# A q store in one transfer, and the sums moved to the middle of a unit

## The chip, the cores and the metric

The kernel runs on one core of a Trainium2 chip. The metric is the device time of one execution in microseconds. Three runs of the kernel before gave 3701.26, 3701.26 and 3703.98, a median of 3701.26.

## What is computed

Eight images of 256 channels and 64x64 pixels go through two layers, all in float32. The first is an attention block whose keys and values come from a 4x4 strided convolution. The second is a linear attention, and only it is touched here (cut to what matters):

```
qkv = einsum('oc,bchw->bohw', w_qkv, x)
dw  = conv5x5_depthwise(qkv, w_dw)
agg = einsum('goi,bgihw->bgohw', w_pw, dw.reshape(B, G, 8, H, W)).reshape(B, G * 8, H, W)
ms  = concatenate([qkv, agg], axis=1)
q, k, v = relu(ms's first 8 of 24), relu(next 8), last 8 with a 1 appended
kv  = einsum('bhnd,bhne->bhde', k, v)
out = einsum('bhnd,bhde->bhne', q, kv); out = out[..., :-1] / (out[..., -1:] + 1e-15)
return x + batchnorm(einsum('oc,bchw->bohw', w_proj, out))
```

So half of the heads ("raw") take q, k and v from qkv itself, and the other half ("agg") from its depthwise 5x5 convolution mixed 8x8 per group.

## The kernel before

Three passes follow each other. **The first pass** computes the attention block and qkv, image by image, and writes qkv to scratch in DRAM: q and k as planes of cells by phase (`planes`), k and v again with tokens on partitions (`kd`, `vd`). Beside that, `conv_weights` (L674) multiplies the convolution's taps by the mixing weights and stores them as matrices (`wtd`), so that the convolution is a matrix product later. For q (j = 0, 1, nine matrices per group) the columns of such a matrix are ordered with the phase f (16 of them) outside and the channel o (8) inside. `wb` is the product (L690) and L698 and L700 store it.

**The second pass** (L1140) goes over 64 units: two halves t, four blocks k of 32 channels, and eight images b, the image innermost. A unit makes

- the raw sums (`summed_raw`, L1361): k times v on TensorE, 32 products of 32 columns, 128x32 (L1367), which read the keys `kq` after their relu and the tokens `vq`;
- the k convolution in three products, `convolve(u, 2)`, `(u, 0)` and `(u, 1)` (L1290, matmuls at L1298), whose results leave PSUM through ScalarE (`both`, L1307), the vector engine (`s`, L1314) and a relu into `r` (L1315);
- the sums of convolved k with v, for the unit before (`summed`, L1377): 32 products of 288 columns (L1384), which read that `r` and the same `vq`, followed by a reduction on GpSimd (`reduced`, L1276, tile `red_agg`) and small work on the vector engine (L1394 to L1401);
- a column of counts for each (`ended_raw`, L1404, and `ended`, L1418), one small product each.

Two units make one convolution of q, for two images at once: nine products (`product`, L1318, matmuls at L1329) are spread over the even and the odd unit that come two units later, in three parts each (`products`, L1439). They read the cells `d` (L1186), differences of columns (`across`, L1227, vector engine) and of rows (`down`, L1240; vector engine L1248 and GpSimd L1249). `finished` (L1334) writes the relu of the result into `r`, a tile with partitions (f, o), four groups h and two images i. `stored` (L1428) writes it to `qd`, which has channels first and phases second, so that each group h of each image is a transfer of its own: eight of 128 KB for two images.

All transfers are issued on SyncE's queue in order. `load_tokens` (L1194) issues one transfer for `kq` and eight for `vq`; `kq` has two buffers and `vq` three, and the third is freed by `summed`. The framework orders each engine's instructions by the order of the code and by when it thinks that their inputs are there, so the issued order can differ from that of the code; `tc.keep_in_program_order` pins an instruction behind the one traced before it on its engine. The small stores and most q stores on SyncE are pinned in this way. PSUM has five buffers for the convolutions (`cv`) and one each for the raw sums, the sums and the counts.

The loop of a unit, without its loads and stores, is this before the change (p = u-1, q = u-2):

```
summed_raw(u)
across(q // 2, 0); down(q // 2, 1)        # even units
summed(p)
convolve(u, 2); paired(u + 1)
products(u, 0); convolve(u, 0); ended_raw(u)
products(u, 1); convolve(u, 1)
ended(p); products(u, 2); positive(u + 1)
```

**The third pass** loads q back (`agg`, L1564), divides and projects. It reads `qd` in the same layout before and after.

Of the kernel before, what the change touches and what calls it, by code (L numbers as in the profile page):

```python
# [27 lines left out]
F32 = mybir.dt.float32  # L28
AF = mybir.ActivationFunctionType
ALU = mybir.AluOpType  # L30
AX = mybir.AxisListType

P = 128
# [8 lines left out]
D0 = C // HEADS  # L42
D1 = 8
# [531 lines left out]
def first_pass(ctx: ExitStack, tc: tile.TileContext, a, fine, planes, x2d, kd, vd, wtd):  # L575
    nc = tc.nc
# [6 lines left out]
    made = ctx.enter_context(tc.tile_pool(name="made", bufs=1))  # L583
# [23 lines left out]
    consts, x_tiles = {}, {}  # L607
# [66 lines left out]
    def conv_weights():  # L674
        for j, half in ((j, half) for j in (2, 3, 0, 1) for half in range(2)):
            n = 6 if j > 1 else 9
            wd = made.tile([P, 8, n, 16], F32, tag="wd", name=f"wd_{j}_{half}", bufs=1)
            src = a.w_big[:, j, 8 * half : 8 * half + 8]
            nc.sync.dma_start(wd[:, :, :4], src.rearrange("p g (n f) -> p g n f", n=4))
            yield  # L680

            tc.keep_in_program_order(nc.vector.tensor_add(wd[:, :, 4:6], wd[:, :, 0:4:2], wd[:, :, 1:4:2]))
            if n == 9:
                tc.keep_in_program_order(nc.vector.tensor_add(wd[:, :, 6:8], wd[:, :, 0:2], wd[:, :, 2:4]))
                tc.keep_in_program_order(nc.vector.tensor_add(wd[:, :, 8], wd[:, :, 4], wd[:, :, 5]))
            for i in range(8):
                g = 8 * half + i
                w = made.tile([P, n * 16, D1], F32, tag="wb", name=f"wb_{j}_{g}", bufs=1)
                tc.keep_in_program_order(
                    nc.vector.tensor_tensor(  # L690
                        w,
                        wd[:, i].rearrange("p n f -> p (n f)").unsqueeze(2).to_broadcast([P, n * 16, D1]),
                        consts["wsmall"][:, j, g].unsqueeze(1).to_broadcast([P, n * 16, D1]),
                        ALU.mult,
                    )
                )
                if n == 6:
                    nc.sync.dma_start(wtd[j][:, g], w.rearrange("p n o -> p (n o)"))  # L698
                else:
                    nc.sync.dma_start(  # L700
                        wtd[j][:, :, g].rearrange("n p o -> p n o"), w.rearrange("p (n f) o -> p n (f o)", n=n)
                    )
                yield


# [348 lines left out]
    n_all = len(order)  # L1054
    todo = {}
    for n in range(n_all + 6):
        now, was = n < n_all, 0 <= n - 1 < n_all
# [12 lines left out]
        if was:  # L1070
            p = order[n - 1]
# [24 lines left out]
        if was and p[2]:  # L1096
            b, s = p[:2]
# [42 lines left out]
def second_pass(ctx: ExitStack, tc: tile.TileContext, a, planes, kd, vd, wtd, kvd, kvg, qd, ahead):  # L1140
    nc = tc.nc
# [16 lines left out]
    def bank(tag, name, bufs=1, n=512):  # L1158
        return psums[tag].tile([P, n], F32, tag=tag, name=name, bufs=bufs)

    units = [(t, k, b) for t in range(2) for k in range(4) for b in range(B)]
    n_all = len(units)
# [120 lines left out]
    def positive(u):  # L1283
        kq = kqs[u]
        tc.keep_in_program_order(nc.scalar.activation(kq, kq, AF.Relu))
        reduced(u, "raw", (kq[:, 0], kq[:, 1]))
# [74 lines left out]
    def summed_raw(u):  # L1361
        kq, vq = kqs.pop(u), vqs[u]
        ps = bank("raw", f"raw_{u}")
        for i in range(8):
            r, c = i // 4, i % 4
            for f in range(4):
                nc.tensor.matmul(  # L1367
                    ps[f * D0 : (f + 1) * D0, :D0],
                    kq[:, r, c, f * D0 : (f + 1) * D0],
                    vq[:, r + 1, c + 1, f].rearrange("p h e -> p (h e)"),  # L1370
                    start=(i == 0),
                    stop=(i == 7),
                )
        raws[u] = ps


    def summed(u):  # L1377
        kt, vq = kts.pop(u), vqs.pop(u)
        kt = kt.rearrange("p q h (n e) -> p q h n e", n=4)
        ps = bank("sums", f"sums_{u}")  # L1380
        for i in range(8):
            par, r, c = i // 4, i // 2 % 2, i % 2
            for h in range(4):
                nc.tensor.matmul(  # L1384
                    ps[h * D0 : (h + 1) * D0, : 36 * D1].rearrange("p (r n e) -> p r n e", r=3, e=D1),
                    kt[:, par, h, 2 * r + c],
                    vq[:, r : r + 3, 2 * par + c : 2 * par + c + 3, :, h].rearrange("p r c f e -> p r (c f) e"),
                    start=(i == 0),
                    stop=(i == 7),
                )  # L1390
        t, k, b = units[u]
        reduced(u, "agg", (kt[:, 0].rearrange("p h n e -> p n h e"), kt[:, 1].rearrange("p h n e -> p n h e")))
        p = small.tile([P, 36, D1], F32, tag="p", name=f"p_{u}", bufs=1)
        nc.vector.tensor_mul(p, ps[:, : 36 * D1].rearrange("p (n e) -> p n e", e=D1), taps[t][:, k])  # L1394
        s = small.tile([P, D1], F32, tag="kv", name=f"kv_{u}")
        nc.vector.tensor_reduce(s, p.rearrange("p n e -> p e n"), AX.X, ALU.add)

        x = small.tile([P, D1, D1], F32, tag="mixed", name=f"mixed_{u}")
        nc.vector.tensor_mul(x, mix[:, 4 * t + k], s.unsqueeze(1).to_broadcast([P, D1, D1]))
        m = small.tile([P, D1 + 1], F32, tag="m", name=f"m_{u}")  # L1400
        nc.vector.tensor_reduce(m[:, :D1], x, AX.X, ALU.add)  # L1401
        maggs[u] = m

    def ended_raw(u):  # L1404
        t, k, b = units[u]
        ps = raws.pop(u)
        col = ps[:, 64:65]
        nc.tensor.matmul(col, reds.pop((u, "raw")), ones, start=True, stop=True)
        m = small.tile([P, D0 + 1], F32, tag="mraw", name=f"mraw_{u}")
        nc.vector.tensor_copy(m[:, :D0], ps[:, :D0])  # L1410
        nc.vector.tensor_copy(m[:, D0:], col)
        mraws[u] = m

    def stored_raw(u):
        t, k, b = units[u]
        tc.keep_in_program_order(nc.sync.dma_start(kvd[b, t][:, k], mraws.pop(u)))
# [11 lines left out]
    def stored(m):  # L1428
        r = quad.pop(m).r
        for i in range(2):  # L1430
            t, k, b = units[2 * m + i]
            for h in range(4):
                c0 = P * t + D0 * k + D1 * h
                put = nc.sync.dma_start(qd[b][c0 : c0 + D1].rearrange("d f n -> f d n"), r[:, h, i])  # L1434

                if 2 * m + i < n_all - 3:
                    tc.keep_in_program_order(put)

    def products(u, part):  # L1439
        m, odd_one = divmod(u - 2, 2)  # L1440
# [7 lines left out]
    for u in range(n_all + 3):  # L1448
        p, q = u - 1, u - 2
        now, was, conv = u < n_all, 0 <= p < n_all, 0 <= q < n_all  # L1450
        if u == n_all - 5:
            next(ahead)
        if 0 < u < n_all:
            summed_raw(u)
        if 1 < u < n_all - 1:
            load_tokens(u + 1)
        if u % 2 and u < n_all:
            load_cells_q(u // 2)
        if was:
            stored_raw(p)  # L1460
        if conv:
            stored_agg(q)
        if u % 2 == 0 and u > 2:
            stored(u // 2 - 2)
        if u == n_all - 3:
            next(ahead)
        if conv and u % 2 == 0:
            across(q // 2, 0)
            down(q // 2, 1)
        if was:  # L1470
            summed(p)
        if now:
            convolve(u, 2)
        if u + 1 < n_all:
            paired(u + 1)
        if u == n_all - 1:
            next(ahead)
        if u == n_all:
            next(ahead)
        if u == n_all + 1:  # L1480
            ahead.send(lambda name: bank("cv", name, 5))
        if conv and u % 2:
            down(q // 2, 2)
        products(u, 0)
        if now:
            convolve(u, 0)
            if u == 0:
                summed_raw(u)
            ended_raw(u)
        if conv and u % 2 == 0:  # L1490
            down(q // 2, 0)
            across(q // 2, 2)
        products(u, 1)
        if now:
            convolve(u, 1)
        if u + 2 < n_all:
            load_cells(u + 2)
        if u == 0:
            load_tokens(2)
            load_weights_q(0, Q_ORDER[:4])  # L1500
            load_weights_q(0, Q_ORDER[4:])
        if was and p == n_all // 2 - 1:
            load_taps(1)
        if was:
            ended(p)
        products(u, 2)

        if u + 1 < n_all:
            positive(u + 1)
        if now and u + B < n_all and 2 <= units[u][2] < 6:  # L1510
            b = units[u][2]
            load_weights(u + B - b, b - 2)
        if conv and units[q][2] >= B - 2 and u < n_all:
            load_weights_q(u - u % 2, Q_ORDER[4:] if u % 2 else Q_ORDER[:4])
# [461 lines left out]
```

## Time and profile before

| what | value |
|---|---|
| median of three runs | 3701.26 us |
| the profiled execution | 3693.05 us |
| its span, first to last instruction | 3691.2 us |
| mean granted TensorE clock | 0.989 |
| TensorE busy | 3574.2 us (97%) |
| vector engine busy | 2316.4 us (63%) |
| GpSimd busy | 1563.9 us (42%) |
| ScalarE busy | 1328.1 us (36%) |
| moved by the DMA engines | 706.52 MB, mean 191 GB/s |
| second pass, from 2000 to 2930 us: DMA share | 0.94 at 268 GB/s |

The busy time is that of instructions; the end of a matmul in the record is modelled, so a busy TensorE can still be short of its peak. "DMA share" is the mean busy share of the 16 DMA engines; in short windows it can be over 1. In rows of waits the columns are the total in us, how often, and the longest. In rows in order of time they are the start, the duration, the engine, the line, the operation, the tiles and how many. SPq is SyncE's queue, where a row shows the time to issue the transfer, not the transfer itself. A float32 matmul stands as two records.

### The profile page before, as it was taken

Reading aid. Unit: us, or ns where it says so; the run is one execution under the profiler, and the core shown is the slowest. Engines: PE = TensorE matmul, PEld = TensorE weight load, DVE = VectorE, ACT = ScalarE, POOL = GpSimd, SP = SyncE. Lnnn points to the kernel's source line nnn. Section 1 sums busy time; section 2 is a strip of 40 time slices with the busy share of each in tenths; the row PEclk is TensorE's granted clock in tenths of the full one; section 3 lists DMA queues with packets and bytes.
Section 4 is the critical chain, followed back from the end, with each engine's and each line's share of the span. In section 5 each row is a group of like instructions: output and inputs, shape, how many; then the busy total and the mean of one; then the engine's idle time right before and its main releaser. Section 6 shows DMA issues by size and latency. Waiting matters only on the chain.

```text
span 3691.2 us, 64550 instructions
## 1 busy us (share of the span) xinstructions
PE 3574.2 (97%) x24738; PEld 1926.9 (52%) x24738; DVE 2316.4 (63%) x3395; ACT 1328.1 (36%) x2729; POOL 1563.9 (42%) x1490
## 2 busy tenths in 40 slices
PE   8999999999999999999998999999999999999998
PEld 4443534435334344353335878877788774333333
DVE  1567576675775766746666777777776675454442
ACT  3344354353443434434551222222222223333322
POOL 2434343343443433434443655555555551222222
PEclk9999999999999999999998999999999998999999
DMA  5336446465474663543647999999999988777773
GB/s 178 104 104 182 133 133 185 125 188 153 132 220 122 160 192 111 162 115 103 164 128 197 270 271 273 267 261 250 272 270 276 254 235 244 221 231 228 223 216 101
DMA packets 632525, 706.52 MB, mean 191 GB/s; under 512 B 84752, under 2 KB 490768, under 8 KB 632208
## 3 DMA queue, kind: packets, MB, share of 16 engines
q1 hardware_dynamic: 632208, 702.31, 67.1%
q8 instruction: 198, 3.24, 0.4%
q14 instruction: 119, 0.97, 0.1%
HBM read 421.44 MB, written 280.69 MB: 190 GB/s over the span
## 4 chain that ended last, share of the span: by engine, by line
PE 74%; DMA 17%; SPq 3%; DVE 3%; issue 2%; ACT 1%; POOL 0%; POOLq 0%; DVEq 0%; ACTq 0%
PE qkv L929 16%; PE p L1699 12%; DMA vq<-v 8%; PE sc L807 7%; PE av L831 6%; PE o L885 6%; PE q L792 6%; PE sr L719 6%; DMA d<-planes 5%; PE cv L1298 3%; PE den L851 3%; PE cv L1329 2%; PE rep L1685 2%; PE sums L1384 2%; SPq L1434 2%
## 5 line engine op out<-in xcount | busy, mean ns | idle before, releaser
L844 POOL TENSOR_TENSOR ej<-e,e 128x512 f32<-128x512 f32 x512 | 682.3, 1362 | 940.0 <-ACT e L813 940.0
L813 ACT ACTIVATE e<-sc 128x512 f32<-128x512 f32 x1024 | 529.5, 607 | 576.6 <-PE sc L807 576.6
L1298 PE MATMUL cv<-w,c 128*128 128x128 f32 x3072 | 384.7, 279 | 8.2 <-DVE eps L1721 6.0
L1298 PEld LDWEIGHTS cv<-w,c 128*128 128x128 f32 x3072 | 361.7, 193 | 38.6 <-issue 36.1
L1709 POOL TENSOR_TENSOR y<-z,xs 128x512 f32<-128x512 f32 x128 | 166.0, 1305 | 448.6 <-ACT z L1707 429.4
L1384 PE MATMUL sums<-vq,r 128*32 128x288 f32 x4096 | 317.9, 420 | 29.4 <-ACT r L1315 27.1
L807 PE MATMUL sc<-q,kk 32*128 32x512 f32 x2048 | 292.9, 639 | 0.0
L929 PE MATMUL qkv<-differences,combined 128*128 128x512 f32 x576 | 291.3, 597 | 0.5 <-POOL differences L902 0.5
L1699 PE MATMUL p<-raw,wp 128*128 128x512 f32 x512 | 246.9, 604 | 6.0 <-ACT z L1707 6.0
L831 PE MATMUL av<-e,vv 128*32 128x512 f32 x2048 | 249.4, 598 | 0.6 <-ACT e L813 0.6
L719 PE MATMUL sr<-x,wsr 128*128 128x256 f32 x1024 | 233.7, 382 | 11.6 <-DMA wsr<-in_w_sr_dram 11.5
L792 PE MATMUL q<-x,wq 128*128 128x512 f32 x512 | 242.2, 594 | 0.0
L1699 PE MATMUL p<-agg,wp 128*128 128x512 f32 x512 | 240.5, 592 | 0.2 <-ACT wp L1637 0.2
L885 PE MATMUL o<-att,wout 128*128 128x512 f32 x512 | 230.4, 593 | 0.0
L719 PEld LDWEIGHTS sr<-x,wsr 128*128 128x128 f32 x1024 | 194.9, 191 | 65.3 <-issue 30.3
L864 DVE STREAM_TRANSPOSE rden<-den 128x512 f32<-128x512 f32 x128 | 90.8, 709 | 208.2 <-PE den L851 202.7
L1384 PEld LDWEIGHTS sums<-vq,r 128*32 128x32 f32 x4096 | 146.0, 112 | 141.5 <-ACT r L1315 42.1
L945 DVE TENSOR_TENSOR whole<-part,qkv 128x512 f32<-128x512 f32 x256 | 172.5, 684 | 67.4 <-ACT part L991 47.3
L800 ACT COPY q<-q 128x512 f32<-128x512 f32 x128 | 75.1, 587 | 372.7 <-PE q L792 372.7
L1329 PE MATMUL cv<-y,w 128*128 128x128 f32 x1536 | 204.1, 279 | 3.4 <-DVE y L1248 2.1
L929 PE MATMUL qkv<-x,wqkv 128*128 128x512 f32 x384 | 188.8, 611 | 5.2 <-ACT e L813 5.2
L1329 PEld LDWEIGHTS cv<-y,w 128*128 128x128 f32 x1536 | 185.9, 193 | 5.0 <-issue 4.9
(159 smaller groups left out, 5588.4 us busy)
## 6 DMA issues: line engine op xcount, KB each, us to landing
planes<-stage SPq DMA_DIRECT2D x128, 578.0 KB
d<-planes SPq DMA_DIRECT2D x128, 578.0 KB
vq<-v SPq DMA_DIRECT2D x256, 256.0 KB
raw<-planes SPq DMA_DIRECT2D x64, 578.0 KB
x<-in_xp_dram SPq DMA_DIRECT2D x64, 512.0 KB
wsr<-in_w_sr_dram SPq DMA_DIRECT2D x128, 256.0 KB
x<-x SPq DMA_DIRECT2D x128, 256.0 KB
k<-turned SPq DMA_DIRECT2D x256, 128.0 KB
```

What stands on the lines that cost most here:

```text
L719: nc.tensor.matmul(ps[:, oc], w[:, ci, oc * P : (oc + 1) * P], strips(b, f // 2)[:, ci, f % 2 * NK : (f % 2 + 1) * NK], start=(f == ci == ...
L792: nc.tensor.matmul(ps, consts["wq"][:, ci, c * P : (c + 1) * P], strips(b, s)[:, ci], start=(ci == 0), stop=(ci == 1),)
L807: nc.tensor.matmul(scs[h], kks[b][rows, c, kc * P : (kc + 1) * P], qs[rows], start=True, stop=True)
L813: nc.scalar.activation(e, scs[h], AF.Exp, scale=D0**-0.5)
L831: nc.tensor.matmul(sums["av"][cols], vvs[b][:, kc, c * P + h * D0 : c * P + (h + 1) * D0], es[h], start=(kc == 0), stop=(kc == 1),)
L844: nc.gpsimd.tensor_tensor(e, es0[h], es1[h], ALU.add)
L885: nc.tensor.matmul(ps, consts["wout"][:, c, oc * P : (oc + 1) * P], att[c], start=(c == 0), stop=(c == 1))
L929: nc.tensor.matmul(ps, w, x, start=True, stop=True)
L1298: nc.tensor.matmul(ps[:, g * P : (g + 1) * P], c[:, i, g, cols], w[:, g, n * P : (n + 1) * P], start=(da == 0), stop=(da == 1),)
L1329: nc.tensor.matmul(out, w[:, g], x, start=True, stop=True)
L1384: nc.tensor.matmul(ps[h * D0 : (h + 1) * D0, : 36 * D1].rearrange("p (r n e) -> p r n e", r=3, e=D1), kt[:, par, h, 2 * r + c], vq[:, r : ...
L1699: nc.tensor.matmul(as_block(ps, i // 2), wp[:, i, oc * P : (oc + 1) * P], block(g, i // 2, i % 2, j), start=(i == 0), stop=(i == 3),)
```

## The change

In the first pass the columns of q's weight matrices are turned round: the channel o outside, the phase f inside. The partitions of the convolved q are then (o, f), which is the order of `qd` in DRAM, and one image's four groups go in one transfer of 512 KB. In the second pass `summed_raw(u)` and `summed(p)` go from the start of a unit to a place between the second and third convolution product, after `products(u, 1)`; `ended_raw(u)` moves behind them.

```
             for i in range(8):
                 g = 8 * half + i
-                w = made.tile([P, n * 16, D1], F32, tag="wb", name=f"wb_{j}_{g}", bufs=1)
...
+                w = made.tile([P, n, P], F32, tag="wb", name=f"wb_{j}_{g}", bufs=1)
+                small_w = consts["wsmall"][:, j, g]
                 if n == 6:
-                    nc.sync.dma_start(wtd[j][:, g], w.rearrange("p n o -> p (n o)"))
+                    v = w.rearrange("p n (f o) -> p (n f) o", o=D1)
+                    big = wd[:, i].rearrange("p n f -> p (n f)").unsqueeze(2).to_broadcast([P, n * 16, D1])
+                    small_w = small_w.unsqueeze(1).to_broadcast([P, n * 16, D1])
                 else:
-                    nc.sync.dma_start(
-                        wtd[j][:, :, g].rearrange("n p o -> p n o"), w.rearrange("p (n f) o -> p n (f o)", n=n)
-                    )
+                    v = w.rearrange("p n (o f) -> p n o f", o=D1)
+                    big = wd[:, i].unsqueeze(2).to_broadcast([P, n, D1, 16])
+                    small_w = small_w.unsqueeze(1).unsqueeze(3).to_broadcast([P, n, D1, 16])
+                tc.keep_in_program_order(nc.vector.tensor_tensor(v, big, small_w, ALU.mult))
...
             t, k, b = units[2 * m + i]
-            for h in range(4):
-                c0 = P * t + D0 * k + D1 * h
-                put = nc.sync.dma_start(qd[b][c0 : c0 + D1].rearrange("d f n -> f d n"), r[:, h, i])
-
-                if 2 * m + i < n_all - 3:
-                    tc.keep_in_program_order(put)
+            c0 = P * t + D0 * k
+            dst = qd[b][c0 : c0 + D0].rearrange("(h d) f n -> (d f) h n", d=D1)
+            put = nc.sync.dma_start(dst, r[:, :, i])
+
+            if 2 * m + i < n_all - 3:
+                tc.keep_in_program_order(put)
...
-        if 0 < u < n_all:
-            summed_raw(u)
...
-        if was:
-            summed(p)
         if now:
             convolve(u, 2)
...
         products(u, 0)
         if now:
             convolve(u, 0)
-            if u == 0:
-                summed_raw(u)
-            ended_raw(u)
         if conv and u % 2 == 0:
             down(q // 2, 0)
             across(q // 2, 2)
         products(u, 1)
         if now:
+            summed_raw(u)
+        if was:
+            summed(p)
+        if now:
+            ended_raw(u)
             convolve(u, 1)
```

## The prediction, made before the changed kernel had run

> **What bounds the kernel now.** I read the busy slices of the page first, then the stretch of the second pass in one-microsecond windows, then the order of one pair of units on SyncE and TensorE, then the list of waits. The change touches the second pass, which is about slices 21 to 32 of 40.
>
> ```profile
> PE   8999999999999999999998999999999999999998
> DMA  5336446465474663543647999999999988777773
> ```
>
> Here the DMA engines are as full as TensorE, and nowhere else are both. So this stage has two candidates for its bound. How long is a unit? The copy at L1307 happens once in each of 64 units:
>
> ```profile
> L1307 ACT COPY both<-cv x64: 569/586/587, 1983.9 to 3021.6; 128x512 f32<-128x512 f32 x64
> ```
>
> 63 steps in 1037.7 us: **16.47 us a unit**. A unit without a wait is seen in the order of TensorE, from one start of the third convolution product to the next:
>
> ```profile
> 2307.93 2.05 PE L1298 MATMUL cv<-w,c 128*128 128x128 f32 x16
> ...
> 2317.78 1.64 PE L1384 MATMUL sums<-vq,r 128*32 128x288 f32 x18
> 2319.13 0.85 PE L1367 MATMUL raw<-vq,kq 128*32 128x32 f32 x63
> ...
> 2322.84 2.05 PE L1298 MATMUL cv<-w,c 128*128 128x128 f32 x16
> ```
>
> That is **14.91 us** (2322.84 - 2307.93), and the unit at 2605.71 to 2620.66 took 14.95; I take 14.92. So 1.55 us of each unit is lost, 63 x 1.55 = 98 us in all: TensorE's work itself allows no more than that to be won. Note that the sums of the unit before run ahead of the first product, where the code puts the raw sums first: the order issued is not always that of the code.
>
> What does TensorE wait for, from 2000 to 2930 us (56.4 units)?
>
> ```profile
> PE sums L1384 <- ACT r L1315: 22.7, 17, 2.9
> PE raw L1367 <- ACT kq L1285: 17.6, 21, 1.1
> PE few L1420 <- POOL red_agg L1280: 4.0, 1, 4.0
> ```
>
> With the smaller rows (2.2, 2.1, 2.0, 1.7, 0.6) it is 52.9 us, of which the first two are 40.3, or 76%. They are waits of the sums for a relu that is only just made. The rest of the 1.55 us (52.9/56.4 = 0.94) is not in the list; the granted clock fell to 0.32 and 0.70 in the windows around such a wait (2304 and 2305 us), which I take to be part of it.
>
> Why are the relus late? The vector engine and ScalarE stand in their own order behind cells that have not landed (DVE L1233 waited 64.1 us for d, GpSimd L1249 156.3 us). So look at the DMA. Columns: five engines' busy us, clock, DMA share, GB/s.
>
> ```profile
> 2307.00:2308.00 1.00, 1.00 (x18) 0.36 (x7) 1.00 (x2) 0.00 (x0) 1.00 (x1) 1.00 1.15 305
> 2309.00:2310.00 1.00, 1.00 (x11) 1.00 (x11) 1.00 (x1) 0.00 (x0) 0.92 (x2) 1.00 0.46 102
> 2311.00:2312.00 1.00, 1.00 (x12) 1.00 (x11) 0.96 (x2) 0.59 (x1) 1.00 (x1) 1.00 0.69 191
> 2314.00:2315.00 1.00, 1.00 (x10) 1.00 (x10) 0.64 (x4) 0.45 (x1) 0.00 (x0) 1.00 0.72 201
> 2316.00:2317.00 1.00, 1.00 (x11) 1.00 (x10) 1.00 (x2) 0.00 (x0) 0.30 (x1) 1.00 1.00 328
> ```
>
> and at what SyncE issued meanwhile:
>
> ```profile
> 2306.43 0.57 SPq L1416 DMA_DIRECT2D kv<-mraw  x1
> 2307.44 0.33 SPq L1426 DMA_DIRECT2D kvg<-m  x1
> 2308.13 5.51 SPq L1434 DMA_DIRECT2D q<-r  x8
> 2313.69 0.60 SPq L1183 DMA_DIRECT2D d<-planes  x1
> 2314.99 0.37 SPq L1197 DMA_DIRECT2D kq<-k  x1
> 2315.46 5.92 SPq L1209 DMA_DIRECT2D vq<-v  x8
> 2321.82 1.22 SPq L1191 DMA_DIRECT2D d<-planes  x2
> ```
>
> Eight stores of 128 KB take 5.5 us of SyncE: it hands over 190 GB/s while the engines can do more, and they run dry. I added up such windows from 2000 to 2960 us. In the 220 that lie around the 28 groups of q stores the mean is 0.63 busy at 168 GB/s, and the idle shares sum to 80.7 us; in the other 740 it is 1.03 at 296.5 GB/s. So outside the q stores the DMA is full, and **each pair of units loses 80.7/28 = 2.9 us of DMA**. The DMA paces the pass, with TensorE close behind.
>
> **What the Trainium skill says.** "DMA: Bandwidth & Descriptors", Rules for kernel authors, advises to merge many small transfers into one large one. The trace agrees, but for SyncE's time to issue, not for the transfer. Its section on the anatomy of one DMA says that the engines do not wait on semaphores; the issuing sequencer does, before it dispatches. That is the risk of this change: one waiting load holds back all later ones. "TensorE: Matmul & The Clock Gate", HAM oscillation, says that idle gaps of TensorE lower its clock, after some 3.4 us; here the clock dips beside waits of 1 to 3 us.
>
> **The change, part by part.**
>
> Weights of q: 32 products on the vector engine (128x1152) keep their size and only walk it in another order, 1.35 us each. Bounds: no change, or twice as long (+43 us of vector time between 860 and 1390 us, where TensorE is the full engine and the vector engine 63% busy; perhaps 5 us would show). I take nothing; the cover is that slack. The weights' stores stay contiguous.
>
> q stores: 256 become 64, of 512 KB. The time to issue one is between 0.38 us (the load of d at L1191 has the same form, 128 partitions by 4 rows, 578 KB, median 376 ns) and 4 x 0.60 = 2.4 us (median of a store now, if it went by bytes). I take 0.4: two of them are 0.8 us for 1 MB where eight took 5.5, and the hole closes. What is queued behind (d, weights, keys) comes 4.7 us sooner.
>
> DMA floor: a unit moves vq 1536 KB, d twice 578, kq 512, q 512, weights 192 and 288, and some 40 of small things, 4235 KB or 4.34 MB; at 296.5 GB/s **14.6 us**. It falls just under TensorE's 14.92.
>
> Sums moved: 64 and 64 records on TensorE, same work. In the new order, from the first product at T: product 1.8, two q products 1.9, product 1.8, one or two q products 1.0 to 1.9, so the raw sums start at T+6.5 to 7.4 and the sums end (0.8 + 4.1 later) at **T+11.4 to 12.3**. The relu of r and that of kq were then made half a unit earlier, so the 40.3 us of waits should go. Next in line are the q products after the first convolution product, which read d and its differences.
>
> The vector and GpSimd work emitted with the sums (1.7 and 3.3 us per unit) moves too. The count of red_agg is wanted one product after; its input is half a unit old. I cost it at nothing: GpSimd is busy 9.6 of 16.5 us. If it stays behind a late d, the 4.0 us row above grows.
>
> Added wait: vq has three buffers, and the load for unit u+2 takes that of u-1, now free at T+11.4 or later. SyncE issues it today at T+7.5 (2315.46 - 2307.93) and T+4.8 in the odd unit (2327.63 - 2322.84). So SyncE will stand there, and behind it are the two loads of d for the q products, both small stores, the q stores and the next cells. The vq load itself is wanted only at T+36, so it loses nothing. The d loads go from T+13.9 to about T+11.4+5.9+0.1 = T+17.4. They took 9.4 us to land (2321.82 to 2331.2), so T+26.8. Their first reader stands two units on at T+31.6, and the differences (1.6 + 1.1 us of vector time) want them by T+29.9: **3.1 us to spare**. While SyncE stands, the engines still have the q stores, cells, weights and keys, about 2.3 MB or 7.5 us.
>
> Sum: the larger floor, 14.92, plus what is left of the losses, 24% of 1.55 = 0.37: 15.3 us a unit. (16.47 - 15.29) x 63 = **74 us** less. Against the profiled execution's 3693.05 (span 3691.2) that is 3619; the median of the runs shown is 3701.26, 8 us above that execution, so 3627.
>
> **The rivals.**
>
> A, half the gain. The hole is moved rather than closed: once SyncE stands until T+11.4, its small stores and the issue of eight vq loads (5.9 us for 1.5 MB, 265 GB/s) leave the DMA short by some 1.5 us a pair, and the vector engine, 12.0 us busy a unit and with 5 PSUM buffers to empty, gives short waits. For: both floors are within 2% of each other[...]. Against: the transfers already handed over cover most of the wait. At 15.8 us a unit, 42 us: 3659.
>
> B, slower. The d loads, issued 3.5 us later, land after T+29.9, and the q products wait in each of 31 pairs. Price: to lose the 74 us takes 2.4 us a pair, so a landing 5.5 us longer than today's 9.4. At 3.5 us of wait a pair, 108 - 74 = +34: 3735. For: GpSimd already waits up to 9.1 us for d. Against: with the q stores short, the queue in front of d is shorter.
>
> C, the store does not get cheaper (2.4 us each). The hole stays, and the waits that the sums lose appear elsewhere: 3695, no change.
>
> **Chances.** Forecast 0.52, A 0.33, B 0.11, C 0.04. A measurement of this kernel can tell 0.2%, 7 us, from no change. Faster 0.85, same 0.04, slower 0.11. The range goes from the floor (3701 - 98, rounded down to 3600) past A to 3690, for A's stalls might be twice what I took; it leaves B and C out.
>
> **What would show it.** Right: q stores of about 0.4 us on SyncE; DMA share of 1 or more while they go; the waits of sums for r and raw for kq gone; L1307's 64 copies 15.3 us apart. Wrong: SyncE idle before vq and a DMA share under 0.8 there (A), q products waiting for d or y (B), issues over 2 us (C), or a longer first pass (the weights).

## The result, and the profile after

The changed kernel took 3657.38 us (median of four, 3644.77 to 3661.01) beside 3702.62 for the kernel before, 45 us or 1.2% less by the medians; the ratio over all runs of both is **0.9865, interval 0.9834 to 0.9897**, faster. Forecast were 3627 and a range of 3600 to 3690; the direction and the range held, the size is 45 of the 74 us expected, and rival A had named 3659. The profiled execution took 3644.77 us against 3693.05, 48.3 less. It was the fastest of its four, 12.6 us under their median, so a length of a unit that is read from one profile stands for the median only to some 0.2 us.

First the length of a unit in the second pass, from the copies at L1307 of the changed kernel (duration of one, then the first and the last start):

```profile
L1307 ACT COPY both<-cv x64: 557/574/586, 1985.4 to 2968.3; 128x512 f32<-128x512 f32 x64
```

63 steps in 982.9 us, **15.60 us a unit** instead of 16.47: 54.8 us won in the loop. It starts 1.5 us later, and from the last copy to the end it is 674.6 us instead of 669.6, so 48.3 remain.

Next the store. These are SyncE's issues in the changed kernel around one group of q stores, and the same time in windows of 1 us (the last two columns are the DMA share and GB/s):

```profile
2329.08 0.56 SPq L1416 DMA_DIRECT2D kv<-mraw  x1
2329.75 0.42 SPq L1426 DMA_DIRECT2D kvg<-m  x1
2330.26 0.96 SPq L1434 DMA_DIRECT2D q<-r  x2
```

```profile
2329.00:2330.00 1.00, 1.00 (x10) 1.00 (x9) 1.00 (x2) 1.00 (x2) 1.00 (x1) 1.00 1.03 307
2330.00:2331.00 1.00, 1.00 (x11) 1.00 (x10) 1.00 (x2) 0.77 (x2) 0.92 (x2) 1.00 0.80 221
2331.00:2332.00 1.00, 1.00 (x11) 1.00 (x11) 0.55 (x1) 0.00 (x0) 0.92 (x2) 1.00 0.83 263
2332.00:2333.00 1.00, 1.00 (x11) 1.00 (x11) 0.43 (x1) 0.00 (x0) 1.00 (x2) 1.00 1.02 324
```

Two issues in 0.96 us where eight took 5.5, and a dip of two windows (shares of 0.80 and 0.83) where there were eight. Added up as before from 2000 to 2960 us, over the windows that touch the issues and the microsecond after them, the idle shares are 18.7 us (80.7 before). As the issues are shorter, that is 95 windows instead of 220; over eight windows from the start of each group it is 24.9 us instead of 81.6. Most of the hole is closed.

The longest waits of the convolutions on TensorE in the changed kernel, from 2000 to 2930 us (total, times, longest):

```profile
PE cv L1329 <- DVE y L1248: 11.0, 8, 2.1
PE cv L1298 <- DVE s L1314: 9.5, 4, 2.7
PE cv L1329 <- DMA d<-planes: 9.2, 5, 4.4
PE cv L1298 <- DVE m L1421: 5.4, 2, 2.7
```

The waits of the sums for r and of the raw sums for kq are gone from the list. In their place stand q products that wait for d or its differences (y), and convolution products that wait for the vector engine (s), which empties a PSUM buffer. They are not spread out: apart from one pair of waits at the start (2017 to 2021 us) and a few short ones they come in seven clusters, near 2166, 2295, 2419, 2541, 2671, 2788 and 2919 us, that is once in eight units. One cluster on TensorE, the idle time before each row in brackets:

```profile
2540.75 1.30 PE L1329 MATMUL cv<-d,w 128*128 128x128 f32 x8 [1.86 <-DMA d<-planes]
2544.11 2.04 PE L1329 MATMUL cv<-y,w 128*128 128x128 f32 x8 [2.06 <-DVE y L1248]
2547.65 3.78 PE L1298 MATMUL cv<-w,c 128*128 128x128 f32 x16 [1.50 <-DVE s L1314]
```

and what SyncE had issued in the two units before it:

```profile
2508.24 6.49 SPq L1177 DMA_DIRECT2D w<-wt  x5
2515.16 3.86 SPq L1209 DMA_DIRECT2D vq<-v  x5
...
2525.30 6.28 SPq L1209 DMA_DIRECT2D vq<-v  x8
2532.75 1.14 SPq L1191 DMA_DIRECT2D d<-planes  x2
```

Once in eight units the nine matrices of the q convolution (2.25 MB) are loaded. After them the load of d was issued 6.1 us before it was wanted (2532.75 to 2538.89); in the next pair it was 14.1 (2563.84 to 2577.91). Outside the clusters TensorE runs at its floor, the time that its own work takes without a wait. From one start of the sums to that of the second next, over a pair of units:

```profile
2304.56 4.08 PE L1384 MATMUL sums<-vq,r 128*32 128x288 f32 x64
...
2319.62 4.07 PE L1384 MATMUL sums<-vq,r 128*32 128x288 f32 x62
...
2333.94 1.40 PE L1384 MATMUL sums<-vq,r 128*32 128x288 f32 x18
```

29.4 us for two units, 14.7 each. The kernel before has to be taken over a pair as well, for of the nine q products four fall to one unit and five to the other. A pair without a wait, from one start of the third convolution product to that of the second next:

```profile
2885.40 2.05 PE L1298 MATMUL cv<-w,c 128*128 128x128 f32 x16
...
2900.95 2.05 PE L1298 MATMUL cv<-w,c 128*128 128x128 f32 x16
...
2915.75 2.05 PE L1298 MATMUL cv<-w,c 128*128 128x128 f32 x16
```

That is 15.55 us with five q products and 14.80 with four, **15.2 us a unit** on the mean; the 14.92 of the prediction is a unit with four. So the floor fell by 0.5 us a unit. Most of that is seen in the sums: raw sums and sums now follow each other in 4.6 us (2319.04 to 2323.62), where before the raw sums split the others and both took 5.1 (2317.78 to 2322.84).

Last, the stretch from 2000 to 2930 us as a whole:

```profile
2000.00:2930.00 930.00, 886.64 (x12689) 777.11 (x12691) 662.57 (x1090) 257.88 (x386) 552.12 (x503) 0.97 0.98 282
```

The DMA share is 0.98 (0.94 before) at 282 GB/s (268 before). Here the DMA is full.

### The profile page after: what moved, and what is told of

The parts are those of the page before. It is cut to its first block, busy times and chain, and to the rows that moved or that the text cites. A ratio compares the mean times of both kernels' runs of the same rounds, so it can differ in the third digit from the quotient of the medians.

```text
span 3642.9 us, 64216 instructions
## 1 busy us (share of the span) xinstructions
PE 3544.9 (97%) x24738; PEld 1944.9 (53%) x24738; DVE 2270.6 (62%) x3395; ACT 1319.4 (36%) x2729; POOL 1544.4 (42%) x1490
## 4 chain that ended last, share of the span: by engine, by line
PE 85%; DMA 8%; DVE 2%; SPq 1%; POOL 1%; issue 1%; ACT 1%; POOLq 0%; DVEq 0%; ACTq 0%
PE qkv L929 16%; PE p L1697 11%; PE cv L1298 8%; PE sc L807 7%; PE av L831 6%; PE o L885 6%; PE q L792 6%; PE sr L719 6%; PE cv L1329 6%; PE sums L1384 5%; PE den L851 3%; DMA vq<-v 2%; DMA d<-planes 2%; DMA raw<-planes 2%; PE rep L1683 2%
## 5 line engine op out<-in xcount | busy, mean ns | idle before, releaser
L1298 PE MATMUL cv<-w,c 128*128 128x128 f32 x3072 | 392.9, 283 | 21.6 <-DVE s L1314 9.5
L1298 PEld LDWEIGHTS cv<-w,c 128*128 128x128 f32 x3072 | 370.9, 198 | 24.0 <-DVE s L1314 16.1
L1315 ACT ACTIVATE r<-s 128x512 f32<-128x512 f32 x128 | 80.8, 631 | 547.2 <-DVE s L1314 519.7
L1384 PE MATMUL sums<-vq,r 128*32 128x288 f32 x4096 | 265.2, 407 | 1.4 <-issue 1.4
L1329 PEld LDWEIGHTS cv<-y,w 128*128 128x128 f32 x1536 | 189.6, 196 | 14.8 <-issue 9.4
L1384 PEld LDWEIGHTS sums<-vq,r 128*32 128x32 f32 x4096 | 155.1, 110 | 76.9 <-issue 2.8
```

The costliest lines, as they stand in the source:

```text
L1298: nc.tensor.matmul(ps[:, g * P : (g + 1) * P], c[:, i, g, cols], w[:, g, n * P : (n + 1) * P], start=(da == 0), stop=(da == 1),)
L1329: nc.tensor.matmul(out, w[:, g], x, start=True, stop=True)
L1384: nc.tensor.matmul(ps[h * D0 : (h + 1) * D0, : 36 * D1].rearrange("p (r n e) -> p r n e", r=3, e=D1), kt[:, par, h, 2 * r + c], vq[:, r : ...
```

## The experiments

**Which half made the gain?** *Only the store* is the kernel before with the first two parts of the change, the turned columns and the one transfer:

```
+                    v = w.rearrange("p n (o f) -> p n o f", o=D1)
...
-            for h in range(4):
...
+            put = nc.sync.dma_start(dst, r[:, :, i])
```

> Only the first half of the change: the turned weight columns and one q store per image; the sums stay at the start of a unit. Theory (store and order each take a loss of their own, and the DMA paced the pass): the idle DMA around the q stores falls from 81 us to under 20, loads land earlier, the waits of sums for r and raw for kq shrink but do not go; 15.9 us a unit, about 3665. Rival (the gain came from the order alone): the hole closes and the time stays over 3690. Rival (the store alone made the gain): 3650 to 3660, as with the whole change.

Measured: 3652.45 us, ratio 0.9866 (0.9850 to 0.9883), 15.81 us a unit in the profile, which is of the slowest of its four runs. The idle share around the q stores fell to 18.8 us (43.1 over eight windows from the start of each group), and the vector engine and GpSimd waited 111 us for d instead of 262: loads land sooner. The waits of the sums shrank with it (same columns and stretch as above):

```profile
PE sums L1384 <- ACT r L1315: 9.6, 6, 2.1
PE raw L1367 <- ACT kq L1285: 8.4, 9, 1.6
```

That is 18.0 us where the kernel before had 40.3. So the store alone gives the whole gain, within the two intervals. The time expected by my theory, 3665, was too high: the rival that said so was right. What it is in the store was not taken apart further, since no run kept eight stores and shortened only their issue. The DMA share over the stretch rose from 0.94 to 0.97, and the rate at a share of 1 by about 1% (284.9 to 288.0 GB/s), so that most of it is the filled hole.

*Only the order* is the kernel before with the last part of the change, and still eight q stores:

```
-        if was:
-            summed(p)
...
         products(u, 1)
         if now:
+            summed_raw(u)
+        if was:
+            summed(p)
+        if now:
+            ended_raw(u)
             convolve(u, 1)
```

> Only the second half of the change: the sums moved to the middle of a unit; q is stored in eight transfers for two images and the weights are as before. Theory: the waits of sums for r and raw for kq go, but the DMA still runs dry for some 2.9 us at each group of q stores, so that the pass stays paced by it: 16.2 us a unit, about 3685. Rival (the order alone made the gain): 3650 to 3660. Rival (the wait before vq costs time of its own): over 3710.

Measured: 3722.15 us, ratio **1.0055 (1.0038 to 1.0071), slower**, against my expectation of a gain.

Its copies at L1307, and its longest waits of TensorE from 2000 to 2930 us:

```profile
L1307 ACT COPY both<-cv x64: 558/584/587, 1987.0 to 3050.0; 128x512 f32<-128x512 f32 x64
```

```profile
PE cv L1329 <- DVE y L1248: 26.2, 12, 4.4
PE cv L1298 <- DVE s L1314: 24.3, 13, 2.7
PE cv L1329 <- DMA d<-planes: 11.0, 5, 5.6
```

16.87 us a unit. The waits of the sums were exchanged for 61.5 us of waits of the convolutions, and the DMA still runs dry at the q stores (90.1 us). SyncE stood idle for some 40 us ahead of vq loads (gaps over 0.3 us between 2000 and 2960 us, added up; the sum changes by 2 or 3 us with how the view merges rows), and for some 9 in the kernel before. Is that wait the cause? *Only the raw sums moved* keeps `summed` at the start, so that vq's buffer is free as early as before:

```
-        if 0 < u < n_all:
-            summed_raw(u)
...
         if now:
+            summed_raw(u)
+            ended_raw(u)
             convolve(u, 1)
```

> The kernel before with only the raw sums (and their count) moved to the middle of the unit; the sums of convolved k stay at the start, so the buffer of vq is free as early as before, and q is stored in eight transfers. Theory (the order-only kernel is slower since SyncE waits for the sums before vq, with everything else queued behind): no loss here, 3690 to 3703. Rival (it is slower because the products of both convolutions then follow each other with five PSUM buffers and no sums between): 3710 or more.

Measured: 3704.66 us, ratio 1.0009 (0.9998 to 1.0019). Idle time ahead of vq is some 14 us, the wait for kq is gone and the wait for r has grown to 54.2. So moving the raw sums costs nothing that can be measured, and the loss of the order belongs to moving `summed`, which frees vq. Then I put the load of d ahead of the waiting vq load, in the order-only kernel:

```
+        if u % 2 and u < n_all:
+            load_cells_q(u // 2)
         if 1 < u < n_all - 1:
             load_tokens(u + 1)
-        if u % 2 and u < n_all:
-            load_cells_q(u // 2)
```

> The order-only kernel (sums in the middle, eight q stores) with the load of the q cells d issued ahead of the tokens in an odd unit. Nothing is left out. Theory (the order alone is slower because the wait before vq stands in front of d; q products waited 37 us for d and its differences): these waits go, 3695 to 3705. Rival (the DMA that runs dry at the q stores sets the pace whatever the order of loads): no change, 3715 to 3730, with the wait at another load.

Measured: 3732.21 us, ratio 1.0091 (1.0073 to 1.0108). TensorE's waits for d and its differences fell to 4.2 us, and others came: raw counts for red_raw 23.9 us, q products for c 18.0. SyncE stood idle ahead of vq for only some 10 us, about as in the kernel before, and the loss is still there. So neither the wait before vq nor its path through d makes the loss. The store-only kernel says the same from the other side: there SyncE stood 116 us ahead of kq loads, and it has the whole gain. That the wait moves to another load is the rival; that the DMA running dry sets the pace, its reason, fits but is not isolated.

**What holds the changed kernel at 15.6?** *q matrices loaded once* leaves the reload out (the matrices of the first group serve all):

```
-            load_weights_q(u - u % 2, Q_ORDER[4:] if u % 2 else Q_ORDER[:4])
+            for ij in Q_ORDER[4:] if u % 2 else Q_ORDER[:4]:
+                wq[units[u][0], units[u][1], ij] = wq[0, 0, ij]
```

> The changed kernel with the matrices of the q convolution loaded once: the reload of 2.25 MB in every eight units is left out, so all groups of q are computed with the matrices of the first. Theory (what remains lost, 0.7 us a unit, is a stall of 5 to 6 us once in eight units, when this reload pushes the load of d behind the q products that need it): the stalls go, 15.0 us a unit, about 3615. Rival (the vector engine and the five PSUM buffers hold TensorE back in every unit): 15.5 us a unit, 3650.

Measured: 3606.37 us, ratio 0.9746 (0.9730 to 0.9762), 51 us less than the changed kernel. The copies stand 14.96 us apart, and of the waits that made the clusters little is left from 2000 to 2930 us:

```profile
L1307 ACT COPY both<-cv x64: 557/578/587, 1984.3 to 2926.6; 128x512 f32<-128x512 f32 x64
```

```profile
PE cv L1329 <- DMA d<-planes: 6.5, 1, 6.5
PE raw L1367 <- ACT kq L1285: 3.9, 2, 3.7
PE cv L1329 <- DVE y L1248: 1.5, 2, 1.4
PE cv L1298 <- DVE s L1314: 0.6, 1, 0.6
```

The 6.5 us are one wait at 2019 us, where the stretch starts. The clusters are gone; neither the vector engine nor PSUM holds TensorE back in an ordinary unit. Is it the burst, or the bytes? Three runs ask. *k matrices loaded once* takes away bytes that come evenly:

```
+        if u:
+            wt[t, k] = wt[0, 0]
+            return
         if g == 0:
```

> The changed kernel with the matrices of the k convolution loaded once: 28 loads of 384 KB (10.5 MB, one each in four units of eight) are left out, so all later groups of k are computed with the matrices of the first. The q matrices are reloaded as before. Theory of bursts (the pass loses where 2.25 MB come within two units, not by its bytes): the stall once in eight units stays, if a little shorter; about 3645. Rival, theory of bytes (every byte less is time won, 51 us for 15.75 MB in the run without the q reload): 34 us less than the changed kernel, about 3620.

Measured: 3629.47 us, ratio 0.9811 (0.9794 to 0.9828): 28 us less, nearer to the theory of bytes (34) than to that of bursts (12). But what the theory of bursts said of the stall holds as well: it is still there. The copies (L1310 here is L1307) and the longest wait of the convolutions:

```profile
L1310 ACT COPY both<-cv x64: 557/580/586, 1987.2 to 2955.1; 128x512 f32<-128x512 f32 x64
PE cv L1301 <- DVE s L1317: 11.4, 5, 2.7
```

That is 15.36 us a unit. At 274.3 GB/s a unit moves 4.21 MB, which at a DMA share of 1 (274.3/0.965 = 284.2 GB/s) take 14.8 us, and TensorE's floor is 14.7. The rest, some 0.5 us a unit, is lost over both floors, and from 2290 us on the longest waits of TensorE still come once in eight units (2293, 2413, 2537, 2660, 2780 and 2905 us).

*q matrices early* keeps the bytes and loads each matrix as soon as its predecessor was read:

```
-        home = w_q.tile([P, len(which), 4, P], F32, tag=f"w0_{len(which)}", name=f"w0_{t}_{k}_{len(which)}")
...
+            wq[t, k, ij] = w_q.tile([P, 4, P], F32, tag=f"w0_{i}", name=f"w0_{t}_{k}_{i}")
...
+        if units[u - 2][2] >= B - 2 and u < n_all:
+            load_weights_q(u, which)
...
```

> The changed kernel with a buffer for each of the nine q matrices, each loaded right after the last product that reads its predecessor, instead of four and five together at the ends of two units. Same bytes, nothing left out. Theory of bursts: five of nine loads come up to 11 us sooner, so d is held up less; the stall of 6.8 us in eight units about halves, about 3635. Theory of bytes: no change, 3650 to 3660.

Measured: 3652.10 us, ratio 0.9870 (0.9844 to 0.9896), no change. It did not spread the burst by much: the nine loads of one group go out between 2478.84 and 2504.53 us, 25.7 us from first to last, where the changed kernel takes 22.6 (2492.10 to 2514.73). *d before the tokens* is the reordering shown above, in the changed kernel:

> The changed kernel with the load of the q cells d issued ahead of the tokens in an odd unit, so that it does not stand on SyncE's queue behind a vq load that waits for the sums. Nothing is left out. Theory (the order on the queue makes d late, not the bytes): the waits of q products for d and of the differences go, 15.1 us a unit, about 3625. Rival (the DMA's bytes bound the pass, share 0.98 with the burst): the stall moves to another load, vq or the weights, and the time stays at 3650 to 3660.

Measured: 3659.84 us, ratio 0.9893 (0.9876 to 0.9909), no gain. As with the order alone, the wait went elsewhere; in the changed kernel GpSimd's copy at L1224 waited 36.5 us for its cells, and now

```profile
POOL c L1224 <- DMA d<-planes: 195.4, 26, 12.0
PE raw L1408 <- POOL red_raw L1280: 18.7, 15, 1.6
```

Of these runs only those with fewer bytes are faster. My theory that the order of the loads makes d late, and that this is the cause, falls. The theory of bursts is not settled: the bytes count wherever they are taken away, for the DMA share is 0.98 over the whole stretch, but the burst is where TensorE stalls, and it stalls there even where both floors leave room. A reload spread over all eight units was not tried.

**What is the order worth, then?** *Store only, q matrices once* joins the first run with the reload left out:

> The store-only kernel (sums at the start of a unit) with the matrices of the q convolution loaded once; as in the earlier run all groups of q use the matrices of the first. Theory (the new order is worth 0.3 us a unit where the DMA keeps up, and loses it again in the stalls of the reload): 15.2 us a unit, 3618 to 3622, some 14 us over the changed kernel without the reload. Rival (the order is worth nothing even then): 3604 to 3610, the same as that kernel.

Measured: 3632.61 us, ratio 0.9817 (0.9800 to 0.9833), 26 us over the changed kernel without the reload (0.9746). So the order does gain 26 us where the DMA has room (a share of 0.93 in this run), and nothing that can be measured where it has none. It is about what TensorE's lower floor gives, 0.5 us a unit or some 33 us in all.

**Faster transfers.** *Rows of cells* lays the k cells out with the partition outermost:

```
-        nc.sync.dma_start(d, planes[b, 2 + t][4 * k : 4 * k + 4].rearrange("g p e -> p g e"))
+        nc.sync.dma_start(d, planes[b, 2 + t][:, 4 * k : 4 * k + 4])
```

> The changed kernel with the scratch of the k cells laid out with the partition outermost, so that a load of k cells (578 KB) reads 128 rows of 4624 bytes instead of 512 of 1156. Bytes and order stay; the first pass's stores of these cells write rows of 1156 bytes instead. Theory (the pass is bound by the time of its transfers: windows with loads of d ran at 285 GB/s and those with vq at 395): a load of k cells takes 1.5 us instead of 2.1, 0.5 us a unit less, about 3625. Rival (the rest is lost to waits in the order of work, not to transfer time): 3650 to 3660.

Measured: 3641.98 us, ratio 0.9847 (0.9820 to 0.9874), which overlaps the changed kernel's.

```profile
2000.00:2930.00 930.00, 893.19 (x12773) 784.71 (x12772) 670.24 (x1102) 260.46 (x388) 552.32 (x506) 0.97 0.98 284
```

The rate rose from 282 to 284 GB/s only. My expectation took the rate of windows for the rate of a kind of transfer; rows four times as long, in loads that are some 13% of the bytes, did not bring it. The same layout in the store-only kernel:

> The store-only kernel (sums at the start of a unit) with the same layout of the k cells. Theory: it gains as well, but TensorE's waits for r and kq then set its pace at some 15.3 us a unit, so about 3635, 10 over the changed kernel with this layout. Rival (the order is worth nothing): the same time as that kernel within 4 us.

Measured: 3654.60 us, ratio 0.9871 (0.9853 to 0.9889): no gain over store only (0.9866), nor clear of the run before; the 3635 that I expected did not come. And both edits together in the changed kernel:

> The changed kernel with both the other layout of the k cells and a buffer for each q matrix, loaded as soon as its predecessor is read. Nothing is left out. Theory (the pass is bound by the sum of its bytes at 282 to 285 GB/s, and neither edit takes bytes away): 3635 to 3650, the time of the better one of the two within what can be measured. Rival (each takes away stalls of its own, which add up): below 3630.

Measured: 3641.98 us, ratio 0.9834 (0.9819 to 0.9849). It is the lowest ratio of the kernels that leave nothing out, but it overlaps the changed kernel's interval, so a better version than the change is not shown.

## Why the prediction was right or wrong

**Right: the store.** Its issue time was taken as 0.4 us; the median is

```profile
L1434 SPq DMA_DIRECT2D q<-r x64: 359/370/1443, 2050.6 to 3004.6; - x64
```

0.37 us. The hole of 80.7 us went down to 18.7, and the store alone carries the whole gain. That the range held rests on this. The sign that I had named, a DMA share of 1 or more while the stores go, did not come: it was 0.80 and 0.83.

**Right: the weights cost nothing.** The product of 128x1152 in the turned order takes as long as before (mean 1351 ns, 1350 before), and the vector engine was busy 1131.4 us in the first 1800 us of either kernel.

**Wrong: the DMA floor, the term that mis-sized the sum.** I put it at 14.6 us a unit, from 4.34 MB at 296.5 GB/s, and so let TensorE set the end. But that rate belonged to windows whose share was 1.03, with the q stores' windows left out. The trace of before had the better figure: 268 GB/s at a share of 0.94 is 285 at 1, and at that the same 4.34 MB take **15.2 us**, which is above TensorE's 14.92. With 15.2 in its place and my 0.37 for what is left of the losses the sum gives 15.6, as measured in the profile (at the median of the four runs it would be some 15.8). After, 281.8 GB/s over units of 15.60 us are 4.40 MB each (I had left out what the third pass loads ahead in the same stretch), and at a share of 1 (281.8/0.983 = 286.7 GB/s) these take 15.3 us; this second figure is only the measured unit times its share, and proves nothing by itself.

**Wrong too: what is left of the losses, and where.** The 0.37 was taken as the part of the old losses that stays. What is lost in the changed kernel is another thing, 0.9 us a unit over TensorE's floor of 14.7: a stall once in eight units, at the reload of the q matrices, which I had spread evenly as 288 KB a unit. The clock adds to it: it stood at 0.5 for some microseconds in five of the seven clusters, and what it fell short of 1 sums to 24 us over the stretch, 15 before.

**Wrong, and covered by luck: TensorE's floor.** 14.92 us is a unit with four q products; a pair takes 15.2 a unit. So of the 1.55 us that I counted as lost 0.3 were work, and without less work on TensorE no more than 63 x 1.27 = 80 us could be won, not 98. The new order then took the floor to 14.7, which I had not seen, and my 14.92 came to lie near it by chance. What I gave for the granted clock beside a wait, 0.32 and 0.70, is TensorE's busy time; the clock, the third figure from the end, is 1.00 there. It did fall elsewhere:

```profile
2177.00:2178.00 1.00, 1.00 (x42) 0.63 (x35) 1.00 (x1) 0.00 (x0) 1.00 (x2) 0.50 1.08 249
2304.00:2305.00 1.00, 0.32 (x2) 0.00 (x0) 1.00 (x2) 1.00 (x2) 1.00 (x2) 1.00 1.05 195
```

Those 15 us are 0.27 us a unit; with 0.94 of waits and 0.3 of the fifth product they come to 1.5 of the 1.55.

**Wrong: what the moved sums are worth.** I counted their 40.3 us of waits as won. More than half of them (40.3 - 18.0) went with the store alone, for they came from late loads; the rest turned into waits for d, for differences and for the vector engine, as the DMA still sets the pace. That the removed wait's successor would be the q products was right.

**Half right: the wait before vq.** It came (SyncE idle ahead of vq some 100 us in the changed kernel, some 9 before), and with eight q stores the move is a loss of 0.55%, the sign that rival B warned of. Rival B's chain, vq delays d and d delays TensorE, is seen in one pair of four, but the two runs with d in front refute it as the cause of the time.

**Rival A** gave 3659, which is near the median, in part by luck: two floors close together was right (15.2 and 14.7), but its small dips of 1.5 us in each pair are not what the trace shows.

**Open:** how the moved `summed` makes the order-only kernel slower, beyond the fact that its place does it and that of the raw sums does not; the wait of SyncE ahead of vq was gone in the run with d in front, and the loss was not. Open too is how much of the rest is bytes and how much the burst, and with it why taking away 10.5 MB won 28 us and 15.75 MB 51: 73% and 89% of the 38.4 and 57.6 us that they take at 286.7 GB/s (MB of 1024 x 1024 bytes here).

## What to carry to other kernels

A stretch with the DMA share at 0.94 has 6% to give, as long as its bytes and its rate at a share of 1 stay as they are: take its floor from the mean rate divided by the mean share, not from the busiest windows. Take the floor of an engine over a whole period of the loop, here a pair of units; one unit alone was 0.3 us short. Eight small stores in a row left the DMA engines short of work here because SyncE took 5.5 us to issue them; joined into two, they were the half of the change that paid. And test the halves apart: here one half made all of the gain and the other alone was a loss.

## What the runs showed of the hardware that was not expected

A store of 512 KB over 128 partitions is issued in 0.37 us, less than one of 128 KB walked as 16 by 8 rows (0.60 us): here the time to issue went by the form, not by the bytes. Loads with rows of 4624 bytes instead of 1156, some 13% of the bytes, raised the rate of the stretch by under 1% (281.8 to 284.3 GB/s). In the kernel before, the granted clock halved for 3.4 us after TensorE had waited 0.84 and 0.96 us within 2.5 us (2174 to 2177 us), but not after a single wait of 2.89 us (2400 to 2403 us).
